# Attention and 32 experts in one kernel: the experts taken in a fixed mixed order instead of from the fullest to the emptiest

## The chip, the cores and the metric

The kernel runs on one core of a Trainium2 chip, in 32-bit floats. The metric is the device time of one execution in microseconds (us), the smaller the better; a kernel's time is the median of several executions. The core has five engines that work beside each other: TensorE (PE in the profile; its weight loads are a row of their own, PEld), VectorE (DVE), ScalarE (ACT), GpSimd (POOL) and SyncE (SP), which here only issues DMAs. Sixteen DMA engines move the data for the queues of SP and POOL.

## The reference

Four sequences of 512 tokens with 512 features go through two layers. The first picks one of four matrices for each token by its token id; the second is a mixture of 32 experts of which each token takes four.

```python
def _L0_ffn_ref(hidden_states, norm_w, gate_w, w13, w2, shared_gate_w, shared_up_w, shared_down_w):
    residual = hidden_states
    h = _rmsnorm(hidden_states, norm_w)
    x = h.reshape(-1, Hd)                       # 2048 tokens x 512
    routed = _moe_core(x, gate_w, w13, w2)
    shared = silu(x @ shared_gate_w) * (x @ shared_up_w) @ shared_down_w
    return residual + (routed + shared).reshape(B, S, Hd)

def _moe_core(x, gate_w, w13, w2):              # E = 32, K = 4, I = 256
    scores = softmax(x @ gate_w.T)
    topk_w, topk_ids = top_k(scores, K)         # weights made to sum to 1
    ...
    buf = ...[sorted_eid, pos].set(x[tok])      # each expert's rows, 512 at most
    g, u = split(einsum('ech,ehf->ecf', buf, w13), 2)
    eo = einsum('eci,eih->ech', silu(g) * u, w2)
    return zeros_like(x).at[tok].add(out_slots * flat_w[order][:, None])

x = x + _L0_xattn_ref(_layernorm(x), ...)
x = x + _L0_ffn_ref(_layernorm(x), ...)
```

How many rows an expert gets depends on the data: 2048 tokens with four choices each make 8192 rows, 256 an expert in the mean.

## The kernel before

Up to about 270 us into the execution the kernel does the first layer, the routing and the shared expert: it normalizes blocks of 128 tokens, multiplies them with the matrix of their expert, chooses each token's four experts, and writes each token's row into a table in DRAM, `s_dram`, with 320 slots for each expert. None of that is touched by the change. The rest, lines 1188 to 1247, is the **stage of the experts**.

The kernel counts the rows of each expert and ranks the experts: rank 0 has the most rows, rank 31 the fewest. `er_i` holds the expert of each rank, and from here on a loop over the 32 ranks does the work (lines 1214 to 1247).

**One rank.** Its first 256 rows (`CM`) are one unit of work: `up_rank` (line 1041) multiplies them with the expert's `w13` into `pg` and `pu` (16 products of 128x128 with 128x256 each, line 1050), ACT takes the silu of `pg`, DVE multiplies it with `pu` to `aT` (line 1057), and `down_rank_by_halves` (line 1071) multiplies `aT` with `w2`. The latter takes seven products of half size instead of eight (a scheme of Strassen's kind, lines 1077 to 1118): it needs sums of `aT` (`s_r`, lines 1075 to 1078, on DVE) and sums of `w2` (`t_r`, line 1068, on DVE), and puts and adds the products into `eo` on ACT (line 1088) and DVE (line 1091). POOL then adds the rows of `eo` to `out` in DRAM (line 1022). The six ranks from 26 on take 240 and from 29 on 228 columns (`LOW`, `width`), and rank 31 goes through a plain `down_rank`.

**A block.** Full experts have more than 256 rows. What is above that is worked off for several ranks at once in a block of 128 rows: ranks 0 to 5 in pairs with 64 rows each, ranks 6 to 17 in fours with 32 rows each (`before`, line 1162). So ranks (0,1), (2,3), (4,5), (6 to 9), (10 to 13) and (14 to 17) share a block, and ranks 18 to 31 are plain. A block is done with the first rank of its group: `up_block` (line 1123) after that rank's `pu`, with the `w13` of all ranks of the group; then ACT and DVE make `a_x`; TensorE turns it (`turn_block_act`, line 1140, `tp_x`), DVE copies it to `aT_x`; `down_block` (line 1148) multiplies it with the `w2` of all ranks of the group. A group's weights must therefore all be there at its first rank.

**Loads.** All go through SP's queue in the order of the loop. `weights` (line 905) loads an expert's `w13` (four DMAs) and `w2` (two), five ranks ahead (`WAHEAD`), into one of six buffers: pool `wts_a` has two, `wts_b` four, and the rank's number modulo 6 picks the pool. `fetch` (line 941) loads the 256 rows as `z`, three ranks ahead (`AHEAD`), in four DMAs of 512-byte pieces; DVE turns them by a 32x32 transposition (line 971, `xT`), and DVE and ACT multiply them with the norm's weights (lines 977 and 981). `fetch_x` (line 950) loads a block's rows; for a four these are twelve DMAs, each group of three behind a read of the expert's number into a register.

**Order on the engines.** Each engine has one stream of instructions. A scheduler of the language places each instruction into these streams when the program is built, by the dependencies and the order of the loop's body; what the kernel orders itself are single pairs (`behind`, `queued`). So a change of the loop's order also changes places within the streams around it.

Of the kernel before, what the change touches and what calls it, by code (L numbers as in the profile page):

```python
# [26 lines left out]
E = 32  # L27
# [14 lines left out]
NX = NXA + (XZ - XA) // XPB  # L42

LOW = ((26, 240), (29, 228))
SL = CM + XWA
NS = E * SL
RW = D + 2 * K + 1
# [12 lines left out]
def tile_xattn_moe(  # L60
# [137 lines left out]
    def behind(ins, other, kind=mybir.DependencyClass.NoSync):  # L198

        tc.add_manual_dep(  # L200
            ins.ins,
            other.ins.name,
            mybir.DependencyInfo(kind, mybir.DependencyReason.DATA),
            reason="order",
        )
# [21 lines left out]
    n = EX * NT  # L227
# [128 lines left out]
    hn_, xT_, aT_, ups, made, held = {}, {}, {}, {}, {}, {}  # L356
# [363 lines left out]
    def number(g):  # L720
# [9 lines left out]
        has = mid.tile([P, GT, K], F32, tag="has", name=f"has{g}")  # L730
        nc.vector.tensor_scalar(has, at, float(SL), None, ALU.is_le)
        nc.vector.scalar_tensor_tensor(at, hs[g][:, :, D : D + K], float(SL), at, ALU.mult, ALU.add)
        js = slice(g * GT, (g + 1) * GT)
# [41 lines left out]
    def ranks():  # L775
# [40 lines left out]
        had = CM  # L816
        for r, n in LOW:
            nc.vector.tensor_scalar(more, rank, float(r), float(had - n), ALU.is_ge, ALU.mult)
# [74 lines left out]
    wts_a = ctx.enter_context(tc.tile_pool(name="wts_a", bufs=2))  # L893
# [9 lines left out]


    def weights(r, e=None):
        wts = wts_a if r % 6 < 2 else wts_b
        if e is None:
            e = expert(r)
        a = wts.tile([P, DC, 2 * I], F32, tag="w13", name=f"w13_{r}")
        rows = w13[bass.ds(e, 1)].rearrange("o (p c) f -> p (o c) f", c=DC)  # L910
        for c in range(DC):
            load(a[:, c : c + 1], rows[:, c : c + 1])
        b = wts.tile([P, IC, D], F32, tag="w2", name=f"w2_{r}")
        rows = w2[bass.ds(e, 1)].rearrange("o (c p) d -> p (o c) d", p=P)
        for c in range(IC):
            load(b[:, c : c + 1], rows[:, c : c + 1])
        return a, b

    s_rows = s_dram[:NS, :].rearrange("(e s) w -> e s w", s=SL)

    on_sync = []

    def load(*args):
        on_sync.append(nc.sync.dma_start(*args))

    def expert(r):
        with queued(on_sync[-4] if len(on_sync) >= 4 else None):
            return nc.sync.value_load(er_i[0:1, r : r + 1], min_val=0, max_val=E - 1)
# [5 lines left out]
    def fetch_parts(z, rows):  # L934
        for q in range(P // SQ):
            load(
                z[q * SQ : (q + 1) * SQ, :, :],
                rows[:, :, q * P : (q + 1) * P].rearrange("o (r b) w -> b (o r) w", b=SQ),
            )

    def fetch(r):

        z = late.tile([P, CM // SQ, P], F32, tag="z", name=f"z_{r}", bufs=AHEAD + 1)
        of = late.tile([P, MJ, RW - D], F32, tag="of", name=f"of_{r}", bufs=AHEAD + 1)
        rows = s_rows[bass.ds(expert(r), 1), :CM, :]
        fetch_parts(z, rows)
        load(of, rows[:, :, D:].rearrange("o (j p) w -> p (o j) w", p=P))
        return z, of

    def fetch_x(rs_, name):  # L950


        m = P // len(rs_)
        z = late.tile([P, P // SQ, P], F32, tag="z_x", name=f"z_{name}", bufs=2)
        of = late.tile([P, 1, RW - D], F32, tag="of_x", name=f"of_{name}", bufs=2)
        num = late.tile([P, XPB], F32, tag="num_x", name=f"num_{name}", bufs=2)
        for i, r in enumerate(rs_):
            rows = s_rows[bass.ds(expert(r), 1), CM : CM + m, :]
            if m == SQ:
                load(z[:, i, :], rows[:, :, :D].rearrange("o s (q c) -> (o q) s c", c=P))  # L960
            else:
                fetch_parts(z[:, i * m // SQ : (i + 1) * m // SQ, :], rows)
            rows = rows.rearrange("o s w -> (o s) w")
            load(of[i * m : (i + 1) * m, 0, :], rows[:, D:])
            load(num[:m, i : i + 1], rows[:, RW - 1 :])
        return z, of, num

    def turn_parts(z, name, after_=None):
        n = z.shape[1] * SQ
        xT = late.tile([P, DC, n], F32, tag=f"xT{n}", name=f"xT_{name}", bufs=2)  # L970
        ins = nc.vector.transpose(  # L971
            xT.rearrange("p c (r b) -> p r c b", b=SQ), z.rearrange("p r (a c) -> p r c a", c=DC)
        )
        if after_ is not None:
            behind(ins, after_)
        h = 2 if n > P else DC
        ins = nc.vector.tensor_tensor(
            xT[:, :h, :], xT[:, :h, :], nwq[:, :h].unsqueeze(2).to_broadcast([P, h, n]), ALU.mult
        )
        for c in range(h, DC):  # L980
            nc.scalar.mul(xT[:, c, :], xT[:, c, :], nwq[:, c : c + 1])  # L981
        return xT, ins

    def tokens_of(num, to, last_):
        ins = nc.vector.tensor_copy(to, num)
        if last_ is not None:
            behind(ins, last_)
        return to
# [48 lines left out]
    def width(r):  # L1037

        return min([CM] + [n for r_, n in LOW if r >= r_])

# [121 lines left out]
    before = {}  # L1162
    for n in range(NX):
        if n < NXA:
            rs_ = range(n * XPA, (n + 1) * XPA)
        else:
            rs_ = range(XA + (n - NXA) * XPB, XA + (n - NXA + 1) * XPB)
        before[rs_[0]] = (n, rs_)

    def block_in(r):  # L1170

        return fetch_x(before[r][1], f"x{before[r][0]}")

    def block_turned(r, rows, after_, first_=None):
        n, rs_ = before[r]
        z, of, num = rows
        xT, _ = turn_parts(z, f"x{n}", first_)
        w = given(of, er_x[:, n : n + 1], f"x{n}", after_)
        m, k = P // len(rs_), len(rs_)
        return xT, w, tokens_of(num[:m, :k], to_x[:m, n, :k], after_)  # L1180

    def block_up(r, turned_, after_):
        n, rs_ = before[r]
        xT, w, to = turned_
        ws = [wt[q] for q in rs_]
        return n, rs_, ws, up_block(xT, ws, f"x{n}", after_), w, to

    AHEAD, WAHEAD = 3, 5
    wt = [weights(0), weights(1)]
    got = {0: fetch(0)}  # L1190
    rows_x = {0: block_in(0)}
    got[1] = fetch(1)
# [2 lines left out]
    wts_b = ctx.enter_context(tc.tile_pool(name="wts_b", bufs=4))  # L1195
# [3 lines left out]
    to_x = last.tile([P, NX, XPB], I32, name="to_x")  # L1199
    part = {}  # L1200

    for r in range(2, AHEAD):
        got[r] = fetch(r)
        if r in before:
            rows_x[r] = block_in(r)

    ahead = {r: [r + WAHEAD] for r in range(E)}
    ahead[0], ahead[1], ahead[2] = [WAHEAD - 1], [WAHEAD], [WAHEAD + 1, WAHEAD + 2]
    for r in range(2, WAHEAD - 1):
        wt.append(weights(r))  # L1210

    turned_x = block_turned(0, rows_x.pop(0), None, muls_s[-1])
    xT, next_ = turn_parts(got[0][0], "0", adds_s[-GT])
    for r in range(E):
        if r + AHEAD < E:
            got[r + AHEAD] = fetch(r + AHEAD)
        if r + AHEAD in before:
            rows_x[r + AHEAD] = block_in(r + AHEAD)
        for q in ahead[r]:
            if q < E:  # L1220
                wt.append(weights(q))
        if r == E - 1:
            need = nc.values_load(over_i[0:1, 0:1], min_val=0, max_val=E)
        if r + 1 < E:
            xT_next, next_ = turn_parts(got[r + 1][0], f"{r + 1}")
        R = w2_sums(wt[r][1], r) if r < E - 1 else None
        aT, made, last_up = up_rank(xT, wt[r][0], width(r), f"r{r}", next_)
        pend = block_up(r, turned_x, last_up) if r in before else None
        wr = given(got[r][1], er[:, r : r + 1], f"{r}", made)
        to = tokens_of(got[r][1][:, :, RW - D - 1], to_all[:, r, :], made)  # L1230
        if r + 1 in before:
            turned_x = block_turned(r + 1, rows_x.pop(r + 1), made)
        if R is not None:
            last_up = down_rank_by_halves(aT, R, wr, to, r)
        else:
            down_rank(aT, wt[r][1], wr, to, width(r), r)
        if pend:
            n, rs_, ws, a, xw, tox = pend
            aTx = turn_block_act(a, f"x{n}")
            eo = weighted(down_block(aTx, ws, last_up), xw[:, 0:1], f"x{n}", "eo_x")  # L1240
            m = P // len(rs_)
            for i, q in enumerate(rs_):
                part[q] = eo[i * m : (i + 1) * m, :], tox[:m, i : i + 1]
        xT = xT_next
        if r in part:
            with queued(adds[f"rank{r}"]):
                push(*part[r], f"rank{r}")
# [3 lines left out]
    with tc.If(need > 0):  # L1251
# [57 lines left out]
        n = E * C // P  # L1309
# [94 lines left out]
```

## Time and profile before

| | us |
|---|---|
| median of 3 executions | 643.95 (643.42 to 644.91) |
| profiled execution, its own time | 647.86 |
| its span, first to last instruction | 646.0 |
| TensorE busy in the span | 608.7 (94%) |
| DVE / POOL / ACT busy | 397.3 / 246.2 / 216.0 |
| stage of the experts, first to last product | 268.76 to 629.17 |
| mean granted TensorE clock | 0.985 |

The groups that cost most in the stage of the experts (line, engine, operation, count; busy time in us and mean ns of one) are the products into `pg` and `pu`, the accumulating DMA issues on POOL and the transposition on DVE:

```profile
L1022 POOL DMA_INDIRECT out<-eo,to_all x64 | 100.5, 1570 | 228.9 <-DVE eo L1091 111.3
L1050 PE MATMUL pg<-xT,w 128*128 128x256 f32 (+2 forms) x512 | 135.2, 377 | 0.0
L1050 PE MATMUL pu<-xT,w 128*128 128x256 f32 (+2 forms) x512 | 114.9, 376 | 0.0
L971 DVE STREAM_TRANSPOSE xT<-z 128x1024 f32<-128x1024 f32 x32 | 65.3, 2041 | 3.8 <-DMA z<-s_dram 3.8
```

A 32-bit product counts twice in these rows, since TensorE runs it in two passes; matmuls are pipelined, so that one lasts 0.38 us while the next of its kind starts 0.216 us after it.

### The profile page before, as it was taken

To read this page: it belongs to the slowest core of one execution; us is meant where nothing else is said; L and a number is where in the kernel's file an instruction comes from. 1 tells how busy PE (TensorE), PEld (TensorE's weight loads), DVE (VectorE), ACT (ScalarE), POOL (GpSimd) and SP (SyncE) were. 2 spreads that over 40 slices of the span, in tenths; PEclk is the share of its full clock that TensorE was granted. 3 is DMA by queue.
4 is the path that set the end of the run, shared out by engine and by line. 5 is a ranking of instruction groups with operands and counts; after the bars stand their busy time and mean duration, and the time that the engine had idled before them with its cause. 6 is when DMAs were issued, how large, how long until landed. Compare 5 with 4: busy or idle time off the path is not lost. (4 is left out here: it accounts for less than half of the span.)

```text
span 646.0 us, 10595 instructions
## 1 busy us (share of the span) xinstructions
PE 608.7 (94%) x2962; PEld 433.5 (67%) x2962; DVE 397.3 (61%) x1113; ACT 216.0 (33%) x390; POOL 246.2 (38%) x217
## 2 busy tenths in 40 slices
PE   5899999999997999999999999999999999999990
PEld 2777767776543444566767687677678888888870
DVE  7655457575725712756667567667668777778730
ACT  2444765764322000122323222322333333333320
POOL 4451101365673555433234324324324232323331
PEclk9999999999997999999999999999999999999996
DMA  7489991335272697698979979979999999999442
GB/s 260 135 309 413 413 415 70 133 118 216 99 269 104 195 375 210 197 319 165 288 154 260 258 151 241 275 160 244 275 265 278 281 261 274 239 247 229 62 55 37
DMA packets 104453, 144.57 MB, mean 224 GB/s; under 512 B 21184, under 2 KB 58048, under 8 KB 101824
## 3 DMA queue, kind: packets, MB, share of 16 engines
q1 hardware_dynamic: 86400, 101.54, 53.6%
q0 software_dynamic: 17984, 42.26, 27.0%
q8 instruction: 26, 0.43, 0.3%
q14 instruction: 43, 0.35, 0.2%
HBM read 79.05 MB, written 66.22 MB: 225 GB/s over the span
## 5 line engine op out<-in xcount | busy, mean ns | idle before, releaser
L1022 POOL DMA_INDIRECT out<-eo,to_all x64 | 100.5, 1570 | 228.9 <-DVE eo L1091 111.3
L1050 PE MATMUL pg<-xT,w 128*128 128x256 f32 (+2 forms) x512 | 135.2, 377 | 0.0
L1050 PE MATMUL pu<-xT,w 128*128 128x256 f32 (+2 forms) x512 | 114.9, 376 | 0.0
L1088 ACT ACTIVATE eo<-po,wt 128x256 f32<-128x256 f32 x124 | 58.6, 474 | 158.5 <-PE po L1085 120.0
L1050 PEld LDWEIGHTS pg<-xT,w 128*128 128x128 f32 x512 | 96.5, 190 | 17.7 <-issue 5.4
L1050 PEld LDWEIGHTS pu<-xT,w 128*128 128x128 f32 x512 | 97.2, 190 | 12.2 <-issue 0.8
L636 POOL DMA_INDIRECT s_dram<-h,slot x64 | 62.2, 973 | 35.4 <-issue 15.4
L458 PEld LDWEIGHTS pp<-xT,held 128*128 128x128 f32 x576 | 66.8, 192 | 8.3 <-issue 5.2
L458 PE MATMUL pp<-xT,held 128*128 128x128 f32 x576 | 68.2, 276 | 1.4 <-DVE xT L450 0.8
L479 PE MATMUL po<-cT,aT 128*128 (+1 forms) x152 | 68.6, 593 | 0.3 <-issue 0.3
L971 DVE STREAM_TRANSPOSE xT<-z 128x1024 f32<-128x1024 f32 x32 | 65.3, 2041 | 3.8 <-DMA z<-s_dram 3.8
L1091 DVE SCALAR_TENSOR_TENSOR eo<-po,wt,eo 128x256 f32<-128x256 f32 x93 | 44.7, 482 | 16.2 <-PE po L1085 9.8
L1057 DVE TENSOR_TENSOR aT_r<-s,pu 128x256 f32<-128x256 f32 (+2 forms) x64 | 26.4, 414 | 41.0 <-PE pu L1050 35.4
L981 ACT ACTIVATE xT<-xT,nwq 128x256 f32<-128x256 f32 x64 | 29.1, 502 | 59.7 <-DVE xT L971 43.1
L479 PEld LDWEIGHTS po<-cT,aT 128*128 128x128 f32 x152 | 27.3, 190 | 27.9 <-issue 27.9
L1068 DVE TENSOR_TENSOR t_r<-w,t_r 128x256 f32<-128x256 f32 x62 | 26.3, 424 | 31.6 <-PE po L1085 29.0
L1085 PE MATMUL po<-t_r,aT_r 128*128 128x256 f32 x124 | 38.1, 389 | 2.0 <-DVE eo L1091 1.5
L605 POOL TENSOR_TENSOR rs<-rs,mhalf 128x2 f32<-128x2 f32 x16 | 11.3, 706 | 74.8 <-DVE rs L604 74.8
L1085 PE MATMUL po<-w,aT_r 128*128 128x256 f32 x124 | 39.7, 401 | 0.0
L389 ACT COPY held<-cT 128x1024 f32 x36 | 36.0, 1048 | 10.3 <-DVE valid L306 10.0
L1085 PE MATMUL po<-t_r,s_r 128*128 128x256 f32 x124 | 37.8, 387 | 0.4 <-DVE eo L1091 0.2
L854 PE MATMUL po<-shw,aT_s 128*128 128x512 f32 x64 | 32.3, 644 | 1.4 <-issue 1.0
(203 smaller groups left out, 765.2 us busy)
## 6 DMA issues: line engine op xcount, KB each, us to landing
w<-in_w SPq DMA_DIRECT2D x192, 256.0 KB
s_dram<-none SPq DMA_DIRECT2D x1, 20840.0 KB
z<-s_dram SPq DMA_DIRECT2D x128, 128.0 KB
h_dram<-h SPq DMA_DIRECT2D x4, 1042.0 KB
cT<-in_ctxT SPq DMA_DIRECT2D x4, 1024.0 KB
out<-none SPq DMA_DIRECT2D x1, 1024.0 KB
s_dram<-h,slot POOLq DMA_INDIRECT x64
out<-eo,to_all POOLq DMA_INDIRECT x64
```

The source lines that it names most:

```text
L389: ins = nc.scalar.copy(held[b][:, h : h + n], cT[:, bass.ds(e, 1), h : h + n].rearrange("p o c f -> p (o c) f"))
L458: ins = nc.tensor.matmul(ups[b][:, f, :], held[b][:, c, f * P : (f + 1) * P], xT_[b][:, c, :], start=(f == 0 and c == 0) if b == 0 else (c ...
L479: ins = nc.tensor.matmul(po, aT_[b][:, f, :], cT[:, bass.ds(off[b], 1), f, :].rearrange("p o f -> p (o f)"), start=(f == 0), stop=(f == DC ...
L636: put = nc.gpsimd.indirect_dma_start(out=table, out_offset=bass.IndirectOffsetOnAxis(ap=index, axis=0), in_=src, in_offset=None,)
L854: ins = nc.tensor.matmul(po, aT[:, f, i * P : (i + 1) * P], w2t[:, f, :], start=(f == 0), stop=(f == IC - 1))
L971: ins = nc.vector.transpose(xT.rearrange("p c (r b) -> p r c b", b=SQ), z.rearrange("p r (a c) -> p r c a", c=DC))
L981: nc.scalar.mul(xT[:, c, :], xT[:, c, :], nwq[:, c : c + 1])
L1022: put = nc.gpsimd.indirect_dma_start(out=out, out_offset=bass.IndirectOffsetOnAxis(ap=dst, axis=0), in_=eo, in_offset=None, bounds_check=T ...
L1050: last_up = nc.tensor.matmul(ps, w13t[:, c, f * P : (f + 1) * P], xT[:, c, :n], start=(c == 0), stop=(c == DC - 1))
L1085: return nc.tensor.matmul(ps, L[i], R[i], start=first_, stop=True, skip_group_check=True)
L1088: nc.scalar.mul(eo[i][:, j, :], ps, wt[:, i : i + 1])
L1091: nc.vector.scalar_tensor_tensor(eo[i][:, j, :], ps, wt[:, i : i + 1], eo[i][:, j, :], ALU.mult, ALU.add)
```

## The change

The loop no longer runs over the ranks 0 to 31 but over a fixed list, `ORDER`. By place in the list it reads: 0 1 2 3 | 18 19 | 6 7 8 9 | 20 21 | 4 5 | 22 23 | 10 11 12 13 | 24 25 | 14 15 16 17 | 26 to 31. Ranks keep their meaning, their widths and their blocks; groups stay together; the two first pairs and the six narrow ranks keep their places. Plain ranks 18 to 25 now stand in pairs between the groups, and the pair (4,5) moves from places 4 and 5 to places 12 and 13. Loads run ahead by places of the list, and the pool of a weight buffer is picked by the place.

```diff
+ORDER = (
+    [0, 1, 2, 3, 18, 19]
+    + [*range(6, 10), 20, 21, 4, 5, 22, 23]
+    + [*range(10, 14), 24, 25]
+    + [*range(14, 18), *range(26, E)]
+)
...
     def weights(r, e=None):
-        wts = wts_a if r % 6 < 2 else wts_b
+        wts = wts_a if (ORDER.index(r) if e is None else e) % 6 < 2 else wts_b
...
-    for r in range(E):
-        if r + AHEAD < E:
-            got[r + AHEAD] = fetch(r + AHEAD)
-        if r + AHEAD in before:
-            rows_x[r + AHEAD] = block_in(r + AHEAD)
-        for q in ahead[r]:
-            if q < E:
-                wt.append(weights(q))
+    for i, r in enumerate(ORDER):
+        for q in ORDER[i + AHEAD : i + AHEAD + 1]:
+            got[q] = fetch(q)
+            if q in before:
+                rows_x[q] = block_in(q)
+        for n in ahead[i]:
+            for q in ORDER[n : n + 1]:
+                wt[q] = weights(q)
+        q = ORDER[i + 1] if i + 1 < E else None
...
-        if r + 1 < E:
-            xT_next, next_ = turn_parts(got[r + 1][0], f"{r + 1}")
+        if q is not None:
+            xT_next, next_ = turn_parts(got[q][0], f"{q}")
...
-        if r + 1 in before:
-            turned_x = block_turned(r + 1, rows_x.pop(r + 1), made)
+        if q in before:
+            turned_x = block_turned(q, rows_x.pop(q), made)
```

The sums, products, DMAs and their sizes are the same as before, and none is added or left out.

## The prediction

> **What bounds the kernel now.** I read first the slices of the page, then TensorE's waits from 350 us on, then the timelines of single engines. The slices say who is full:
>
> ```profile
> PE   5899999999997999999999999999999999999990
> PEclk9999999999997999999999999999999999999996
> ```
>
> From slice 18 (some 275 us) to slice 39 TensorE is busy in every slice at the full granted clock. The chain of waits is no help: it breaks off at POOL's last two DMA issues (0.4% of the span). What TensorE still waits for in the stage:
>
> ```profile
> PE po L1085 <- DVE eo L1091: 1.5, 4, 0.4
> PE po L1085 <- issue: 0.4, 1, 0.4
> PE pp_x L1130 <- DMA w<-in_w: 0.2, 1, 0.2
> ```
>
> So the stage lasts as long as TensorE's own stream, in its order; another order of experts can gain only what TensorE idles, and loses whatever it makes TensorE wait. TensorE's timeline (start, length, idle before) shows what one of these waits costs:
>
> ```profile
> 398.62 0.59 PE L1050 MATMUL pu<-xT,w 128*128 128x256 f32 x2
> 399.52 0.70 PE L1085 MATMUL po<-t_r,aT_r 128*128 128x256 f32 x2 [0.30 <-DVE eo L1091]
> 400.06 3.19 PE L1050 MATMUL pu<-xT,w 128*128 128x256 f32 x14
> ```
>
> Two passes take 0.43 us from start to start (six take 1.29, 397.33 to 398.62). Here they take 0.90 and then 0.54: a wait shown as 0.30 costs 0.47 + 0.11 = 0.58 us. By the same subtraction the waits at 378.91, 426.33 and 474.15 cost 0.64 each, the one at 447.08 0.72, and the wait for weights at 450.99 0.26. Elsewhere in the stage the start-to-start times show 0.48 (282.63), 0.21 (293.64) and, around the first four at 345 to 352, 1.2. All together 5.4 us: that is the most that could be gained.
>
> **The work itself: nothing.** Plain ranks run at 10.0 us (their `pu` start at 484.28, 494.30, 504.31). A pair's block adds 3.58 + 0.22 + 1.87 = 5.7 us of TensorE (from 328.63, 333.61, 339.11), a four's 3.57 + 0.31 + 1.86 = 5.7 (from 355.75, 361.58, 365.11). There are three of each in both kernels, and the narrow ranks stay. After TensorE's last product (629.17) come 16.9 us of pushes and landings; the last six ranks are the same, so this tail only shifts with TensorE.
>
> **The loads: slack, so nothing.** SP's queue is the other thing that is moved: a rank's six weight DMAs and five row DMAs move with it, a pair's 12 and a four's 12 block DMAs too. In plain ranks SP starts a set of weights every 9.55 us (465.0 to 579.55 in 12 ranks), against 10.0 on TensorE. A four takes 48.4 us on SP (387.89 to 436.24) against 47.6 on TensorE (355.75 to 403.17 to 450.99), because its block rows hold SP from 374.95 to 387.89. So before, three fours in a row used up the lead: a four's last weights started 10.2, 7.2 and 6.5 us before its block (345.55, 396.02, 444.49), and at 6.5 the wait for weights appears. In the new order the pair (4,5) is no longer queued ahead of the first four: SP saves its stretch of 10.5 us (292.70 to 303.19), TensorE 5.7, and the lead there becomes 15.0. On to rank 10 the four and two plain ranks cost SP 67.5 and TensorE 67.6, the pair and two plain ranks 4 x 9.55 + 10.5 = 48.7 and 4 x 10.0 + 5.7 = 45.7: a lead of 12.1 is left, and more if TensorE waits on the way. The 0.26 goes.
>
> **The small waits on DVE's adds: a little less.** Here the listing of the built programs counts, engine by engine. Ahead of a block's rank DVE turns the block's rows (`xT_x`, 1.09 + 0.69 us in the rows at 397.14 and 398.26), before the last add of the previous rank (399.00), and TensorE's last half product waits for that add. Ahead of ranks 10 and 14 the new stream has this transposition behind the last add: 0.58 and 0.72 go. Ahead of rank 4 (behind rank 21) it is now in front of it: the same kind comes new; bounds 0 and 0.72 from the rows above, and I take 0.64. The other five stay, in the same places between the same instructions.
>
> **The order at rank 4: the cost of this change.** In the old DVE stream rank 4's own work (two `aT`) and the transposition of rank 5's rows (`xT`) stand ahead of the block's `a_x`. In the new listing, at rank 4 alone, they stand behind it:
>
> ```
> DVE  t4_r4 | a_x2 | aT_x2<-tp_x | xT_5 transposition | xT_5 x norm | aT_r4 | aT_r4 | s1_r4 ...
> PE   pp_x x8 | tp_x x2 | pg of rank 5 x1 | po of rank 4 x4 ...
> ```
>
> That DVE holds back what stands behind a waiting instruction is seen in the old trace at this block (TensorE's product, ACT's silu, then DVE):
>
> ```profile
> 328.63 3.65 PE L1130 MATMUL pp_x<-w,xT_x 128*64 128x512 f32 x16
> 332.39 0.38 ACT L1135 ACTIVATE s_x<-pp_x 128x256 f32<-128x256 f32 x1 [6.52 <-PE pp_x L1130]
> 328.29 0.86 DVE L1057 TENSOR_TENSOR aT_r<-s,pu 128x256 f32<-128x256 f32 x2
> 332.81 0.42 DVE L1137 TENSOR_TENSOR a_x<-s_x,pp_x 128x256 f32<-128x256 f32 x1 [3.65 <-ACT s_x L1135]
> 333.35 0.28 DVE L1075 TENSOR_TENSOR s_r<-aT_r 128x128 f32<-128x128 f32 x1
> 334.29 0.42 DVE L1145 COPY aT_x<-tp_x 128x256 f32<-128x256 f32 x1
> ```
>
> `s_r` was ready at 329.15 and ran after `a_x`, 4.2 us later; TensorE had other products then. Now it has none: it turns `a_x`, and its next instruction needs the rows of rank 5. From the end of the block's product (332.28 there) I count: `a_x` done at +0.95 (333.23); two transpositions and the copy, +0.42 from the transposition's start (361.58 to 362.00) and 0.42 long, done at +1.84; then
>
> ```profile
> 352.75 2.02 DVE L971 STREAM_TRANSPOSE xT<-z 128x1024 f32<-128x1024 f32 x1
> 354.80 0.69 DVE L977 TENSOR_TENSOR xT<-xT,nwq 128x512 f32<-128x512 f32 x1
> 355.41 0.87 DVE L1057 TENSOR_TENSOR aT_r<-s,pu 128x256 f32<-128x256 f32 x2
> ```
>
> 2.74 us from the transposition's start to the end of the second row: +4.6. Until then TensorE has done 0.22 us: 4.4 lost. Its next four products of rank 4 stand as at 344.96 to 347.48 (one right after `aT`, then those with `s_r`), which took 2.52 for 4 x 0.43: 0.8 more. Together 5.2. Low end: 4.0, if the four products find their inputs and the copy starts at once. High end 6.0, if the first product also has to wait for ACT's two parts of `xT` (0.91 in the row at 354.86). Behind this wait stand the rest of rank 4 on DVE, its adds and its two pushes on POOL; nothing there is later than TensorE itself. SP's loads gain 5 us of lead by it.
>
> Sum: 643.95 - 0.58 - 0.72 - 0.26 + 0.64 + 5.2 = **648.2 us**, or 652.1 on the profiled execution's base of 647.86 (span 646.0 and 1.9 around it), which is 3.9 above the median; only the difference is carried over. With the low ends (643.95 - 1.56 + 0 + 4.0) it is 646.4, with the high ones and nothing gone (0.72 + 6.0) 650.7.
>
> **The clock.** Of one idle stretch of this length the old trace tells more:
>
> ```profile
> 198.27 0.47 PE L667 MATMUL pl<-ident,lT 128*128 128x128 f32 x1 [4.75 <-ACT lT L661]
> 198.00:202.00 4.00, 3.73 (x6) 1.64 (x7) 2.35 (x13) 1.50 (x2) 0.96 (x1) 0.50 0.00 0
> ```
>
> After 4.75 us without a product the granted clock (third value from the end) was 0.50. In the windows around it it is 0.85 (194 to 198), 0.50 and 0.79 (202 to 206): 1.2 + 4.0 + 1.7 = 6.9 us at half clock, of which TensorE worked 5.4 and lost 2.7. At rank 4 the two transpositions cut the idle time into 0.9 and some 3.3 us, with 0.2 of work between; the shortest idle time in the trace with a drop is 4.75, the longest inside the stage without one 0.44, so the row does not decide. It is nearer to 4.75 as a whole, but neither piece is that long, and I take no drop; a drop would cost 2.7 to 3.4 (half of 6.9). The Trainium skill, "TensorE: Matmul & The Clock Gate", section "Part 1: The HAM clock gate (the "warmup" mystery)", speaks against this change here: the clock halves after an idle window of about 3.4 us, and the windows run freely. By that rule a piece of 3.3 us would just miss a window unless 0.2 us of work count as idle; with a drop the sum would be near 651, without it stays 648.
>
> **Rivals.** A drop of the clock (0.13): 648.2 + 3.1 = 651.3. For it: 4.2 us with next to no work. Against: no piece of 4.75.
>
> Late weights (0.06): if SP's queue falls behind by more than I count, the blocks of ranks 10 and 14 wait. At a lead of 6.5 the wait is 0.3; each us of lead lost below that is one of wait at both, so 3 us short at both give 648.2 + 6 = 654. Against: SP's own 9.55 and the wait at rank 4.
>
> Faster (0.06): the mix could bring all rows and weights so early that DVE never runs late and all waits but the one at rank 4 go. Price 5.4 less at most; with the low end of rank 4 that is 643.95 - 5.4 + 4.0 = 642.6. It decides from the point where over 4.0 of the 5.4 go. For it: DVE waited 3.8 us for `z` before. Against: that wait ended none of TensorE's, and four of the waits lie between instructions that stand as before.
>
> No change (0.06): the wait at rank 4 is paid in part only, 1 to 2 us, because something that I count on TensorE there was slack. Then the gains of 0.9 to 1.56 take it up: 644. Against: TensorE shows no slack at this block before.
>
> **How the numbers follow.** My case has 0.69, with 646.4 to 650.7; the time is its 648.2. The range of 8 in 10 reaches up to 651.5 to take in the clock, and down to 645.6. What can be told from no change is 0.2%, 1.3 us. Slower by more: 0.69 + 0.13 + 0.06 = 0.88; within 0.06; faster 0.06.
>
> **What would show it.** At rank 4's block (some 415 to 425 us) the `tp_x` product with an idle time of 0.9 us in front, then a `pg` product with 3 us or more that ends with DVE's `xT`; in TensorE's waits a new line for `xT`; no line for weights at a block. The granted clock tells of the drop. I am wrong if that `pg` follows `tp_x` closely, or if waits at ranks 10 and 14 are larger than the one at rank 4.

## The result, and the profile after

The changed kernel takes 648.95 us (648.39 to 649.73, six executions) against 644.16 (643.41 to 645.04, six) for the kernel before: a ratio of 1.0075, 95% interval 1.0062 to 1.0088, or 4.8 us more. The prediction was 648.2 from 643.95, 4.25 us more. The span of its profiled execution is 647.4 us, the mean granted clock 0.985. Line numbers are 8 higher than before.

The slices of the page of the changed kernel:

```profile
PE   5999999999997999999999999979999999999992
PEclk9999999999997999999999999989999999999997
```

Against the same two rows of before the stage has one new mark in each: a 7 of TensorE in slice 27, counted from 1 as in the prediction (some 421 to 437 us), and an 8 of the clock in the same slice. All else in the stage is full as it was. TensorE's waits from 350 us on (total, times, longest) name the cause:

```profile
PE pg L1058 <- DVE xT L985: 3.2, 1, 3.2
PE po L1093 <- DVE eo L1099: 1.4, 4, 0.4
PE tp_x L1151 <- DVE a_x L1145: 0.9, 1, 0.9
```

The first and third line are new, the wait for weights is gone. TensorE's timeline there (start, length, idle before):

```profile
418.12 3.65 PE L1138 MATMUL pp_x<-w,xT_x 128*64 128x512 f32 x16
422.71 0.44 PE L1151 MATMUL tp_x<-ident,a_x 128*128 128x128 f32 x2 [0.94 <-DVE a_x L1145]
426.36 1.10 PE L1058 MATMUL pg<-xT,w 128*128 128x256 f32 x2 [3.21 <-DVE xT L985]
427.25 1.06 PE L1093 MATMUL po<-w,aT_r 128*128 128x256 f32 x2
428.10 1.06 PE L1093 MATMUL po<-t_r,s_r 128*128 128x256 f32 x2
428.96 1.09 PE L1093 MATMUL po<-w,aT_r 128*128 128x256 f32 x2
429.89 0.60 PE L1093 MATMUL po<-w,s_r 128*128 128x256 f32 x2
430.32 0.59 PE L1058 MATMUL pg<-xT,w 128*128 128x256 f32 x2
```

The block's product takes 3.58 us from start to start and could have been followed at 421.70; `tp_x` starts 1.01 later. It takes 0.22, so the `pg` of rank 5 could have started at 422.93 and starts 3.43 later. The five pairs from 426.36 to 430.32 take 3.96 instead of 5 x 0.43 = 2.16, 1.80 more. Together 6.24 us. DVE's timeline shows the order that does it:

```profile
422.23 0.42 DVE L1145 TENSOR_TENSOR a_x<-s_x,pp_x 128x256 f32<-128x256 f32 x1 [6.61 <-ACT s_x L1143]
423.19 0.42 DVE L1153 COPY aT_x<-tp_x 128x256 f32<-128x256 f32 x1 [0.53 <-PE tp_x L1151]
423.53 1.96 DVE L979 STREAM_TRANSPOSE xT<-z 128x1024 f32<-128x1024 f32 x1
425.52 0.69 DVE L985 TENSOR_TENSOR xT<-xT,nwq 128x512 f32<-128x512 f32 x1
426.13 0.75 DVE L1065 TENSOR_TENSOR aT_r<-s,pu 128x256 f32<-128x256 f32 x2
```

DVE stood still for 6.61 us in front of `a_x`, although rank 5's rows had landed at 411.8: its stream did not let it turn them first. The windows (length, busy time of PE, PEld, DVE, ACT, POOL, then the granted clock) tell why the five pairs were slow:

```profile
420.00:424.00 4.00, 2.21 (x12) 0.52 (x8) 1.24 (x3) 0.38 (x1) 1.24 (x1) 1.00 0.98 225
424.00:428.00 4.00, 1.64 (x4) 1.40 (x5) 3.96 (x11) 0.91 (x2) 0.00 (x0) 0.81 1.06 320
428.00:432.00 4.00, 4.00 (x15) 2.76 (x15) 1.45 (x5) 1.42 (x3) 0.00 (x0) 0.77 1.19 226
```

(0.19 + 0.23) x 4.00 / 0.5 = 3.4 us at half clock, which cover the slow pairs.

The whole stage, by the time from the first `pu` of a rank to the first `pu` of the next rank in the kernel's own order, for the ranks that changed (us, worked out from the starts in the traces; e1, e2, e5 and e7 are experiments below):

```
rank            before   after     e1      e2      e5      e7
 4 (pair)        15.89   23.14   17.60   15.89   22.23   21.48
 5               11.23   10.02   10.02   10.82   10.02   10.02
 9                9.59   10.11   10.02   10.02    9.61   10.02
10 (four)       17.16   16.16   16.16   16.16   17.17   16.16
13               9.58   10.06   10.02   10.02    9.59   10.02
14 (four)       17.56   16.16   16.16   16.16   17.16   16.16
19              10.02   11.12   11.13   10.02   10.02   11.12
21              10.02    9.58    9.58   10.02   10.02    9.58
rank 0 to 31   350.28  355.57  349.85  348.41  355.00  353.84
```

Other ranks agree within 0.15 us, and a kernel repeats itself: the kernel before took 350.36, 349.92 and 350.47 in three more executions (e4, e9, e10), the changed one 355.50 (e8). The change adds 5.3 us: 6.8 at rank 4 (rank 21's 9.58 counted with it; a pair of products of 0.43 moves across that boundary), less 0.5 at ranks 9 and 10 and 0.9 at 13 and 14. The 1.2 us that were lost ahead of the first four (at rank 5 before) are now lost at rank 19 (1.1), which stands there.

So the stage grew by 5.3 and its first `pu` starts 0.8 later (272.97 against 272.21), yet the two spans differ by 1.4. The rest is at the end: from TensorE's last product to the end of the span it was 16.9 us before (629.17 to 646.05) and is 12.2 now (635.21 to 647.44). POOL's timeline has the last adds (start, length, idle before). In the kernel before:

```profile
627.10 1.55 POOL L1022 DMA_INDIRECT out<-eo,to_all  x1 [0.30 <-issue]
633.17 1.56 POOL L1022 DMA_INDIRECT out<-eo,to_all  x1 [4.52 <-ACTq L1251]
635.04 1.61 POOL L1022 DMA_INDIRECT out<-eo,to_all  x1 [0.30 <-issue]
```

And in the changed kernel:

```profile
629.10 1.56 POOL L1030 DMA_INDIRECT out<-eo,to_all  x1 [0.47 <-ACT eo L1096]
634.66 1.56 POOL L1030 DMA_INDIRECT out<-eo,to_all  x1 [4.00 <-ACT eo L1025]
636.52 1.63 POOL L1030 DMA_INDIRECT out<-eo,to_all  x1 [0.30 <-issue]
```

Rank 31's rows were ready at 628.18 and 629.90 before; their adds started 5.0 and 5.1 us later. What the page names there (a branch of ACT) had long been done. What came just before 633.17 was the landing of the add issued at 627.10, at 632.4. Now the adds start 0.4 and 0.6 us behind their rows. Before I return to this, the experiments.

### The profile page after: what moved, and what is told of

It is laid out like the page before. It is cut to its first block, busy times and chain, and to the rows that moved or that the text cites. A ratio compares the mean times of both kernels' runs of the same rounds, so it can differ in the third digit from the quotient of the medians.

```text
span 647.4 us, 10587 instructions
## 1 busy us (share of the span) xinstructions
PE 610.9 (94%) x2962; PEld 434.6 (67%) x2962; DVE 395.9 (61%) x1113; ACT 216.4 (33%) x390; POOL 246.8 (38%) x217
## 4 chain that ended last, share of the span: by engine, by line
PE 61%; issue 9%; DMA 8%; POOL 7%; DVE 6%; SPq 5%; another core or an unknown queue 2%; ACT 1%; POOLq 0%; DVEq 0%
PE pu L1058 14%; PE po L1093 13%; PE pg L1058 13%; PE po L487 5%; PE pp L466 4%; POOL s_dram L644 4%; SPq L932 4%; DMA w<-in_w 3%; DMA z<-s_dram 2%; PE pg L847 2%; PE pp_x L1138 2%; PE po L862 2%; PE pu L847 2%; DMA out<-eo,to_all 2%
## 5 line engine op out<-in xcount | busy, mean ns | idle before, releaser
L1099 DVE SCALAR_TENSOR_TENSOR eo<-po,wt,eo 128x256 f32<-128x256 f32 x93 | 44.7, 481 | 16.9 <-PE po L1093 9.3
L397 ACT COPY held<-cT 128x1024 f32 x36 | 36.0, 1047 | 10.2 <-DVE valid L314 9.9
```

Of the source, the lines that this page charges most:

```text
L397: ins = nc.scalar.copy(held[b][:, h : h + n], cT[:, bass.ds(e, 1), h : h + n].rearrange("p o c f -> p (o c) f"))
L1099: nc.vector.scalar_tensor_tensor(eo[i][:, j, :], ps, wt[:, i : i + 1], eo[i][:, j, :], ALU.mult, ALU.add)
```

## The experiments

The chips of the experiments are not all alike: the kernel before takes 634 to 641 us on one kind and 643 and more on the other (see the last section). Ratios are to the kernel before on the same chip.

**e1: two instructions put back.** The order of ranks stays as changed; `a_x` is tied behind the last sum of its rank (`s4`). By the listing this moves `a_x2` and `aT_x2` on VectorE, and on TensorE `tp_x` behind them; the other five blocks already have that order.

```diff
-        nc.vector.tensor_tensor(s4, a12, s2, ALU.subtract)
+        sums.append(nc.vector.tensor_tensor(s4, a12, s2, ALU.subtract))
...
-        nc.vector.tensor_tensor(a, s, pp[:, I:], ALU.mult)
+        blocks.append(nc.vector.tensor_tensor(a, s, pp[:, I:], ALU.mult))
...
         if pend:
+            behind(blocks[-1], sums[-1])
```

> The changed kernel with two VectorE instructions put back: at rank 4's block a_x2 and aT_x2 stand behind rank 4's own s4, as the other five blocks have them, and so behind the transposition of rank 5's rows; all else stays. Theory A (these two instructions, ahead of xT_5, cost the stage 1.01 + 3.43 + 1.80 = 6.24 us, the clock drop in it about 1.0): 649.0 - 6.2 = 642.7 us, under the kernel before by 1.4; no wait of tp_x or pg at rank 4's block above 0.3 us, granted clock 1.00 there. Rival B (the mixed order pays in its loads or in what it collides with, and the wait only shows it): 647 or more, with another wait in place of this one. Rival C (the adds to the output, each rank's behind the landing of the rank's before, set the end): TensorE ends 6 us earlier, the kernel gains 4 or less, about 645.

Measured: 634.15 against 636.24, ratio 0.9961 (0.9946 to 0.9976); again on the other kind of chip (e12) 644.17 against 647.06, 0.9951 (0.9926 to 0.9976). TensorE's timeline at rank 4:

```profile
407.52 3.65 PE L1140 MATMUL pp_x<-w,xT_x 128*64 128x512 f32 x16
411.10 0.70 PE L1058 MATMUL pg<-xT,w 128*128 128x256 f32 x2
411.64 0.59 PE L1093 MATMUL po<-w,aT_r 128*128 128x256 f32 x2
412.07 0.60 PE L1093 MATMUL po<-t_r,s_r 128*128 128x256 f32 x2
412.81 0.70 PE L1093 MATMUL po<-w,aT_r 128*128 128x256 f32 x2
413.35 0.59 PE L1093 MATMUL po<-w,s_r 128*128 128x256 f32 x2
413.78 0.38 PE L1153 MATMUL tp_x<-ident,a_x 128*128 128x128 f32 x2
```

`pg` follows the block's product at once, `tp_x` comes later and waits for nothing. The stage is 5.7 us shorter than in the changed kernel and 0.5 shorter than before, so the loss was these two instructions, with `tp_x` between them on TensorE. Rival B falls, and C with its 645: nearly all of what TensorE saved arrived at the end (639.76 for the changed kernel in e8, on another chip of this kind, less 634.15 is 5.6). Rank 4 keeps 1.3 (17.60 + 9.58 against 15.89 + 10.02): 0.6 is the wait on DVE's add that the prediction put at 0.64, and in the rows above three starts come 0.11, 0.31 and 0.11 late. The time is 2.1 us below the kernel before, and the stage accounts for 0.5 of it; the profiled executions of e1 and of the kernel before on this chip (e4) took 634.60 and 634.38. So the other 1.6 stands in the unprofiled executions of the kernel before, and what made them longer is not shown.

**e2: the pair left early.** Fours still alternate with plain ranks, but the pair (4,5) keeps places 4 and 5.

```diff
+ORDER = [0, 1, 2, 3, 4, 5, 18, 19, *range(6, 10), 20, 21, *range(10, 14), 22, 23, 24, 25, *range(14, 18), *range(26, E)]
```

> The mixed order with the pair (4, 5) left at places 4 and 5: 0-5, 18, 19, 6-9, 20, 21, 10-13, 22-25, 14-17, 26-31. Fours still alternate with plain ranks. Here the built VectorE stream has a_x2 and aT_x2 behind aT_r4. Theory A: 643.2 us (the kernel before less about 1 of small waits), no wait of pg on xT above 0.5 at rank 4. Rival B (the mixing of fours and plain ranks is the cost): 647 or more. Rival C (the adds set the end): between 643 and 645, with the last adds 3 us or more behind the rows that they add.

Measured: 632.11, ratio 0.9928 (0.9901 to 0.9955); again on the other kind of chip (e11) 642.91, 0.9931 (0.9903 to 0.9959). It beats both kernels, by more than theory A's 1 us under the kernel before: 4.1. The stage is 348.41, 1.9 less than before: ranks 10 and 14 gain as in the changed kernel, rank 5 loses 0.8 instead of 1.2, and rank 4 is back at 15.89. These 0.8 us do not belong to the first four: the sixth place of the list loses them in before, after, e1, e2 and e3, whichever rank stands there (5, 19, 19, 5, 19) and whatever follows; the other 0.4 appear only where the first four follows it. Why that place loses is not known. So the mixing itself was worth 1.9 us of the stage, and moving the pair cost more than that. The other 2.2 of the 4.1 lie outside the stage, and whether the mixing made them is as open as in e1.

**e3: only the pair moved.** The old order with ranks 18 and 19 at places 4 and 5 and the pair behind them.

```diff
+ORDER = [0, 1, 2, 3, 18, 19, *range(4, 18), *range(20, E)]
```

> The order before with two places exchanged: ranks 18 and 19 run at places 4 and 5, and the pair (4, 5) behind them at places 6 and 7; then 6-17, 20-31. No four is moved from its neighbours. The built VectorE stream has a_x2 and aT_x2 ahead of xT_5, as in the changed kernel. Theory A: the kernel before plus 6.2, 650.2 us (649.4 to 651), with tp_x at 0.9 and pg at 3.2 us of idle time and a granted clock near 0.8 for some 4 us behind it. Rival B: within 1 us of the kernel before, 644.2.

Measured: 640.49 against 636.24, ratio 1.0068 (1.0046 to 1.0091), with the same idle times (0.94 and 3.21) and 3.4 us at half clock. The stage has 5.2 us more than before and the time 4.25, where theory A had 6.2. So no four needs to move for the loss, and the loss comes with the built order.

**e5: the old order of ranks, the two instructions ahead.** At rank 4 alone the loop's body issues the block's `a_x` and `aT_x` first, then the transposition of rank 5's rows.

```diff
+        ahead_x = r == 2 * XPA
...
+            def next_(last_up):
+                early["pend"] = block_up(r, turned_x, last_up)
+                early["aTx"] = turn_block_act(early["pend"][3], f"x{early['pend'][0]}")
+                early["xT"], ins = turn_parts(got[r + 1][0], f"{r + 1}", made_x[-1])
+                return ins
...
```

> The kernel before in its own order of ranks; only at rank 4's block a_x2 and aT_x2 are put ahead of the transposition of rank 5's rows on VectorE, and tp_x ahead of rank 5's first pg on TensorE, as the changed kernel has them. Theory A: rank 4 to rank 6 takes some 6 us more, with 0.9 us idle ahead of tp_x, 3.2 ahead of pg, and 3.4 us at half clock behind it: the kernel before plus 6.0 (ratio 1.0095, 1.008 to 1.0105). Rival D (part of it comes back in the 1.2 us that the kernel before loses ahead of its first four, 345 to 352): plus 4.8, ratio 1.0075. Rival B (the new order of ranks costs, not the two instructions): ratio 1.000 to 1.002.

Measured: 640.64 against 636.69, ratio 1.0070 (1.0039 to 1.0100). TensorE at rank 4:

```profile
323.82 0.44 PE L1147 MATMUL tp_x<-ident,a_x 128*128 128x128 f32 x2 [1.00 <-DVE a_x L1139]
327.67 1.19 PE L1050 MATMUL pg<-xT,w 128*128 128x256 f32 x2 [3.42 <-DVE xT L977]
328.66 1.06 PE L1087 MATMUL po<-w,aT_r 128*128 128x256 f32 x2
```

This puts the same loss into the kernel before by those two instructions (and `tp_x`) alone: rank 4 takes 22.23 instead of 15.89. But rank 5 gives 1.2 back (10.02 instead of 11.23) and rank 14 0.4, so the stage has 4.6 more. Rival D was right and my first figure of 6.0 too high.

**e7 and e8: the clock.** e8 is the changed kernel again. In e7 it has seven products more in the idle time, which nothing reads.

```diff
+        if r == XPA * 2:
+            for k in range(7):
+                ins = nc.tensor.matmul(
+                    p12[:, 1, :], ident, wt_now[0][:, k % DC, :HD], start=True, stop=True, skip_group_check=True
+                )
+                behind(ins, fill["tp"])
...
```

> The changed kernel with seven more products of 128x256 (the identity by weights, into rank 4's first sum, which the next product overwrites) on TensorE between tp_x and rank 5's first pg at rank 4's block: 3.0 of the 3.2 us of idle time are filled with work that nothing waits for. Theory (the idle time halves the granted clock behind it, worth 1.0 of the 1.8 us that the products behind it lost, the other 0.8 being inputs that come late): granted clock 1.00 in the stretch behind, the changed kernel less 1.0, ratio to the kernel before about 1.006. If the late inputs were nothing: less 1.8, 1.0047. If the clock falls for another reason: no change, 1.0075, and 0.8 in the windows again. The wait itself (4.4 us) stays in all.

> The changed kernel again, beside the others on their chip. Theory A: rank 4's place as before (0.94, 3.21, a clock near 0.8 for 8 us of windows behind it), ratio to the kernel before 1.0075 less what the kernel before loses by late adds on this chip: 1.004 to 1.0075.

Measured: e8 639.76 against 636.69, ratio 1.0054 (1.0032 to 1.0077); e7 637.65, 1.0023 (1.0004 to 1.0041), 2.1 us less than e8, so nearer to the 1.8 of the second case (late inputs nothing) than to the theory's 1.0. The windows of e8:

```profile
412.00:416.00 4.00, 0.66 (x3) 0.46 (x4) 3.44 (x6) 0.91 (x2) 0.00 (x0) 0.91 1.13 261
416.00:420.00 4.00, 3.98 (x12) 2.71 (x13) 2.35 (x10) 0.95 (x2) 0.00 (x0) 0.66 1.08 371
```

The same windows of e7:

```profile
412.00:416.00 4.00, 3.64 (x17) 2.96 (x18) 3.43 (x6) 0.91 (x2) 0.00 (x0) 1.00 1.05 287
416.00:420.00 4.00, 4.00 (x19) 3.34 (x19) 2.82 (x12) 1.40 (x3) 0.00 (x0) 1.00 1.18 235
```

DVE is as busy in the first window of both; only TensorE's idle time was filled, and the clock stays at 1.00. In TensorE's timeline of e7 the idle time is 0.26, and the pairs behind it go at full speed:

```profile
412.38 3.19 PE L1095 MATMUL po<-w,ident 128*128 128x256 f32 x14
415.82 0.67 PE L1058 MATMUL pg<-xT,w 128*128 128x256 f32 x2 [0.26 <-DVE xT L985]
416.33 0.59 PE L1103 MATMUL po<-w,aT_r 128*128 128x256 f32 x2
416.76 0.59 PE L1058 MATMUL pg<-xT,w 128*128 128x256 f32 x2
```

Rank 4 goes from 23.18 (e8) to 21.48: 1.70 of the 1.80 us were the clock. One reservation: in e7 a `pg` stands between the first two products of rank 4, which gives DVE 0.43 us more. So the split between clock and late inputs could be off by as much as late inputs would have cost without it.

**e4, e9, e10, and the lag of the adds.** The kernel before, profiled three more times.

> The kernel before, profiled once more, for its end: in the execution shown the last product of TensorE ended at 629.17 and the span at 646.0, 16.9 us later, and the last add of rows left 5.1 us behind its rows; in the changed kernel these are 12.2 and 0.6. If the lag was that execution's own: 12 to 13 us from the last product to the end, and a span near 642. If the old order makes it (Rival C, adds behind adds): 16 us or more again, and the unprofiled times of the kernel before hold it too.

> The kernel before, one more profiled execution. Its unprofiled times on this chip spread over 633.8 to 640.6 with a median 2.3 above the profiled one of e4. Theory C' (late adds make the spread): its time less 634.4 is its lag at the last add less 1.1, within 0.7 us. Rival: a time above 635.5 with a lag of 1 us or less and the same length of TensorE's stage, so the rest is elsewhere.

> As the run ahead of it: theory C' has time less 634.4 equal to the lag at the last add less 1.1, within 0.7 us; the rival has a longer time with a lag of 1 us or less.

e4 took 634.4 us (span 632.6), with 13.2 us from the last product to the end, between its two outcomes; e9 and e10 fell on the other kind of chip and took 647.2 and 648.0, with 15.1 and 15.2. POOL's end in e9 names the releaser rightly:

```profile
626.20 1.55 POOL L1022 DMA_INDIRECT out<-eo,to_all  x1 [0.30 <-issue]
632.53 1.56 POOL L1022 DMA_INDIRECT out<-eo,to_all  x1 [4.78 <-DMA out<-eo,to_all]
```

With the start of each add less the end of its rows on ACT or DVE (the lag; of a rank's two adds the larger), and the time from the last product to the end of the span:

```
                     before   e9    e10    e4    e5    e3   after   e8    e7    e1   e12   e2   e11
lag at rank 16          3.8   2.3   2.7   2.7   3.1   2.5    2.2   0.8   2.5   2.9   3.0  2.4   1.7
lag at rank 26          8.5   8.2   7.7   6.4   8.3   6.4    3.0   2.8   4.4   4.9   2.7  3.9   3.1
lag at the last add     5.1   3.4   3.4   1.1   2.9   1.1    0.6   0.7   0.8   1.7   0.5  0.9   0.5
last product to end    16.9  15.1  15.2  13.2  14.8  13.6   12.2  12.7  12.7  13.8  12.9 13.0  12.7
```

The last row less the one above is 11.6 to 12.5 everywhere (13.9 in e6, below). In the old order (the first five columns) the plain ranks 18 to 25 follow each other, in e3 still 20 to 25: TensorE needs 10.0 us for one, and two adds that wait for the two before need as much or more (517.69 to 527.72 and 558.19 to 569.80 in the execution shown before). There the lag grows from rank 16 to 26, and the narrow ranks work off only part of it. In the mixed orders each block gives POOL 5.7 us, and the lag is 0.3 to 0.4 again at ranks 4, 5, 10, 11, 14 and 15 of the changed kernel. At the last add the two groups overlap (1.1 to 5.1 and 0.5 to 1.7). The theory's sum for e9 and e10 (time less 634.4) can't be made across chips.

**e6: fewer adds.**

```diff
-        push(eo[1].rearrange("p j d -> p (j d)"), to[:, 1:2], f"rank{r}")
+        if not 16 <= r < 26:
+            push(eo[1].rearrange("p j d -> p (j d)"), to[:, 1:2], f"rank{r}")
```

> The kernel before without the add of the second half of the rows of ranks 16 to 25 (that part of the output is left out); products, loads and order stay. In the runs so far each rank's adds on GpSimd wait for the rank's before, and in the old order they fall behind their rows from rank 16 to 26, by 6.4 and 8.5 us at most in the two profiled executions; 1.1 and 5.1 of it are left at the last add. The unprofiled times of the kernel before on that chip went from 633.9 to 640.4 (median 636.2) where the profiled one took 634.4. Theory C' (the lag left at the end makes this spread): a lag under 1 us at the last add, ratio 0.9965 and times within 1.5 us of each other. Rival (the spread is from elsewhere): ratio 1.000, as wide a spread.

Measured: 635.99 against 636.69, ratio 1.0001 (0.9980 to 1.0022): the rival's ratio, not the 0.9965 of theory C'. The middle half of its times lies within 635.7 to 636.6, that of the kernel before within 634.8 to 637.4, but three of twelve still reach 637.5 to 640.6, far outside the 1.5 us of the theory. Its lag at the last add is 1.0 as wanted, yet the end came 7.7 us behind the last landing, against 5.4 to 5.5 in before, after, e1 and e4, for a reason I don't know, so the lag was not all that changed. Theory C' found no support; where the spread of the unprofiled times comes from stays open.

**e11 and e12: e2 and e1 again.**

> The mixed order with the pair (4, 5) at places 4 and 5 once more, in a new call (chips differ: the kernel before took 634.4 on one and 647 to 648 on another). In all profiles so far the time from TensorE's last product to the end of the span is 11.6 to 12.5 us plus the lag of the last add behind its rows (but for e6). Theory: TensorE's stage is 2.0 us shorter than in the kernel before, and the lag at the last add is 1 us against 1.1 to 5.1: in all 2 to 6 us less, about 4.5, ratio 0.993 (0.990 to 0.997). If the first call's gain was that chip's own: ratio 0.997 to 1.000.

> The changed kernel with the two VectorE instructions put back once more, beside e11. Theory: TensorE's stage 0.5 us shorter than in the kernel before, the lag at the last add 1.7 against 1.1 to 5.1: 0 to 4 us less, about 2.3, ratio 0.9965, and about 2 us behind e11.

Both ratios came as expected (0.9931 and 0.9951, given above); e12 is 1.3 us behind e11 where about 2 was expected, and its lag at the last add was 0.5, not 1.7.

## Why the prediction was right

**TensorE's own stream bounds the stage: right.** Each gain or loss of the stage that was followed up stood in its waits or its clock.

**The order at rank 4: right in place and mechanism, the sum by two errors against each other.** Forecast 4.4 idle and 0.8 for late inputs, 5.2; measured 1.01 + 3.43 = 4.44 and 1.80, 6.24. (The +1.84 in it is 1.79 by the rows that it names; in the changed kernel it was 1.84.) e1 and e5 show that the two instructions and `tp_x` make it, without any other part of the change. The mis-sized term is the 0.8: I took the four products from a place where they had waited for `s_r`, while here DVE was through with `s_r` before TensorE wanted it. e7 points to 0.1 for it, and to 1.7 for the clock, which the sum had at nothing. That the 0.8 stood in for half of the clock is luck: the stage grew by 5.3 us where the sum has 4.3, and the time by 4.8.

**The clock: wrong.** I assumed no drop, and gave one 2.7 to 3.4 us, the size of the drop at 197 us. It came in each of the four executions with this wait (after, e3, e5, e8), lasted 3.4 us each time, half as long as that one, and cost 1.7. The Trainium skill, "TensorE: Matmul & The Clock Gate", section "Part 1: The HAM clock gate (the "warmup" mystery)", gives about 3.4 us of sustained work until full clock is back. At rank 4 the runs agree with it, while near 197 us the half clock lasted 6.8 us (before, after) and 10.2 us (e9 to e12). It gives one idle window of the same length for the drop; here pieces of 0.94 and 3.21 us with 0.4 of work between were enough. I had compared the length of single pieces; the traces show that this is the wrong measure. In all of them each stretch between two changes of the clock is a whole number of 3.413 us long, so the clock is set on a fixed grid. With TensorE's busy time (first value) in single steps of this grid, and the short time behind each, in e8 at rank 4, in e9 and in e12:

```profile
411.86:415.28 3.42, 0.44 (x2) 0.20 (x2) 2.85 (x4) 0.28 (x1) 0.00 (x0) 1.00 1.13 241
415.29:415.40 0.11, 0.00 (x0) 0.00 (x0) 0.11 (x1) 0.11 (x1) 0.00 (x0) 0.50 1.45 341
191.77:195.18 3.41, 1.59 (x4) 0.48 (x3) 0.69 (x1) 0.00 (x0) 2.80 (x3) 1.00 0.59 232
195.18:195.30 0.12, 0.12 (x1) 0.00 (x0) 0.00 (x0) 0.00 (x0) 0.07 (x1) 0.50 0.21 70
628.57:631.98 3.41, 1.61 (x4) 0.33 (x2) 0.00 (x0) 1.31 (x2) 2.10 (x2) 1.00 0.20 20
631.99:632.20 0.21, 0.00 (x0) 0.00 (x0) 0.00 (x0) 0.00 (x0) 0.21 (x1) 1.00 1.44 88
```

In e8 the clock is at half before the `pg` at 415.78 starts, and 0.44 us of work did not prevent it. In e12 it fell at 195.07 with no idle time over 1.14 us in the step before, so, other than the page has it, neither an idle step nor one long idle time is needed. Over all 14 traces each of the 24 steps at full clock with at most 1.59 us of busy time was followed by half clock, and none with 1.61 or more (the busy times rest on modelled ends); at half clock 2.9 us or more brought the full clock back, and 2.7 or less did not. At rank 4 some step holds at most 1.4 us wherever the grid lies, so the drop was bound to come; in e7 each holds 2.4 or more.

**The small waits: right.** Ranks 9 and 10 together, and 13 and 14, became 0.5 and 0.9 shorter (forecast 0.58, and 0.72 + 0.26), and the new one ahead of rank 4 is 0.58 (forecast 0.64).

**The loads: no wait, but the lead was wrong.** The last weights started 7.4 us ahead of the first four's block (343.13 to 350.56) where 15.0 was forecast, then 12.3 and 9.2 ahead of the next two. The 12.3 is near the forecast 12.1 by luck, since TensorE's wait at rank 4 lies before it. SP reached them only 2.4 us earlier than before, though it was spared 10.5 us of block rows. Why, I have not settled; 7.4 was still enough.

**The tail only shifts: wrong.** It follows the lag of the adds. That lag is longer in the old order at rank 26 (6.4 to 8.5 us against 2.7 to 4.9 in the mixed ones); how much of it is left at the last add changes from execution to execution. I read the tail from one execution, whose lag of 5.1 us was the largest of five in the old order. The stage's 5.3 us and a tail 0.5 to 4.7 us shorter make the difference of a pair of executions, but for where the stage starts; the 4.8 us measured lie nearer to the stage alone. The six unprofiled executions of the kernel before have no trace, so their lag is not known.

**The work: right.** Plain ranks run at 10.02 in all kernels. Of the rivals, the clock's came true in kind and not in size; late weights, faster and no change did not.

## What to carry to other kernels

When a loop's order changes, compare the built streams of each engine, before and after: at one place two instructions that wait for TensorE came ahead of 3 us of work that waited for nothing, and that cost more (6.2 us) than the new order gained elsewhere (1.4). One `behind` takes it back (e1), and another order that doesn't provoke it is better still (e2). And look for a second chain beside the one that bounds the kernel: the adds of a plain rank need about as long as TensorE, and what they lag behind at the last add, 0.5 to 5.1 us here, comes on top of the 11.6 to 12.5 us of the end.

## What the runs showed of the hardware

The runs fall into two kinds; whether the chip makes them or something else in its runs is not shown. The stage of the experts took the same time in both (350.28 and 350.36 for the kernel before), but in one kind ACT's copy of the routing scores comes late. ACT's timeline of the kernel before:

```profile
197.95 0.27 ACT L661 COPY lT<-pc 128x128 f32<-128x128 f32 x1 [8.35 <-remote]
```

The same instruction in e4, of the other kind:

```profile
190.15 0.27 ACT L661 COPY lT<-pc 128x128 f32<-128x128 f32 x1 [1.39 <-PE pc L653]
```

TensorE waited for it 2.4 to 6.2 us in before, after and e9 to e12, never in e1 to e8. There the clock drops at 194 to 198 us, ahead of the copy, for 6.8 or 10.2 us, and the stage of the experts begins 10 us later. The profile calls the releaser remote; what it is stays open.
